# A four-layer kernel on one core: the second expert run and layer 2 put into one instruction stream

## The chip, the cores and the metric

The kernel runs on one core of one Trainium2 chip. The core has five instruction streams: PE (TensorE, matrix products), DVE (VectorE), ACT (ScalarE, functions by table), POOL (GpSimd) and SP (SyncE, which here issues DMAs). Each executes its own instructions in the order in which they were built; semaphores make one wait for another. SBUF is the working memory with 128 partitions. PSUM takes PE's results in eight banks, each holding 128x512 float32 numbers. The metric is the device time of one launch in microseconds; the lower the better.

## What is computed

Eight sequences of 512 tokens with 128 features (`x[0]` to `x[7]`, float32) stay in SBUF and pass through four layers. Each layer has a feed-forward half, an attention or mixing part, and again the feed-forward half. Every part works on a layer-normed copy of `x`, and a feed-forward half adds half of its result. The change touches layer 1's feed-forward (a mixture of experts, which runs twice) and all of layer 2, with the first feed-forward of layer 3. The reference, cut to those:

```python
# layer 1, ffn: 16 experts of width 64, the 4 best of each token
scores = jax.nn.sigmoid(xf @ gate_w.T)
...                     # best 2 of 4 groups, then best 4 experts in them
topk_w = topk_w / (topk_w.sum(-1, keepdims=True) + 1e-20) * SCALE
cw = (jax.nn.one_hot(topk_idx, E) * topk_w[..., None]).sum(1)
hg = jnp.einsum('nh,eih->nei', xf, Wg)
hu = jnp.einsum('nh,eih->nei', xf, Wu)
act = jax.nn.silu(hg) * hu
y = jnp.einsum('nei,ne,ehi->nh', act, cw, Wd)
shared = jax.nn.silu(xf @ Ws_g.T) * (xf @ Ws_u.T) @ Ws_d.T
return x + (y + shared)

# layer 2, ffn: inputs and weights rounded to a 4-bit grid by blocks of 16
h = jax.nn.silu(fp4_linear(x, w_gate)) * fp4_linear(x, w_up)   # width 352
return fp4_linear(h, w_down)

# layer 2, mixing: gates by 16x16 blocks, a product and a sum along the tokens
a = jnp.exp(-8.0 * gate_a * jax.nn.softplus(a_param))
p = jnp.cumprod(a, axis=1)
return p_prefix * jnp.cumsum(x * gate_x * multiplier / p_prefix, axis=1)

# layer 3, ffn: relu(x @ w1 + b1) @ w2 + b2, width 512
```

`cw` is called "shares" here: one number for each token and expert, zero where the expert was not chosen. All 16 experts are computed for all tokens, and the shares select.

## The kernel before

`_run_stages` calls one method after the other: `l0_ffn`, `l0_attn`, `l0_ffn`, `l1_ffn`, `l1_attn`, `l1_ffn`, `layer2`, `l3_attn`, `l3_ffn`. A Tile scheduler turns what they emit into one instruction stream for each engine. The order of emission is the priority, and the scheduler reorders by its own model of when operands are ready. Inside a `with self.in_order(...)` block the named engines keep the order of emission. Each stage opens its own SBUF and PSUM pools and closes them at its end, so a stage's first tiles wait until the stage before has released the space. A tile name with `bufs=n` is a ring of n buffers: the n+1st use waits for the readers of the first.

**The experts.** `routed(b)` prepares sequence b: it norms it (`norm`, lines 322 to 338), transposes it on PE (`transposed`, 421) into `xT`, and `route` computes the scores and the ranks in 26 DVE operations with two POOL operations between them (`ranks`, 947 to 953). Line 1005 ends the shares. Then `routed` splits them into a leading and a trailing part (876, 878), copies both four times side by side on POOL (881), transposes the result on PE (887) and rounds it to fp32r on ACT (891). `experts(b)` does the nine wide products. Eight steps take two experts each, the ninth is the shared one. In each step PE computes `pg` and `pu` (two 128x512 products), ACT takes the silu of `pg` into `act` (913), DVE multiplies by `pu` (914). For each pair of steps PE spreads the shares of four experts over 128 partitions with two small products `pw`, and DVE multiplies `act` by `pw` (922). The product `po` adds up all nine in one bank. At the end the result is copied (929), transposed (932) and added (934, 431). `routed(b + 1)` is emitted between the steps of `experts(b)`.

PSUM holds two banks each of `pg`, `pu` and `pw`, and one each of `po` and `mm`. All products are float32; each 128x512 one is two records of PE in the trace.

Constants that later stages need are prepared between the steps. `attention_constants` runs in the first expert run, `layer2_constants` (with the load of layer 2's weights, their rounding and nine transposes) in the second.

**Layer 2.** `layer2` cuts the three kinds of work into pieces with a slot each: `rounded_ffn` (twice), `recurrence` (two sequences at a time) and `relu_ffn`, layer 3's first feed-forward. A piece's slot is its table entry (`_ROUNDED_FFN`, `_RECURRENCE`, `_RELU_FFN`) plus a start and a step for each sequence (`_STARTS`, `_STEPS`); all pieces are sorted by slot and emitted in that order. Within one rounded ffn, `fp4_in` takes block maxima and scales (1015 to 1027, the last on POOL), `fp4_out` rounds with ACT, two DVE operations and POOL (1040 to 1043), `gated` computes silu and product (1187, 1188), then come transposes (1203) and the down product. A recurrence uses three of ACT's function tables in turn: sigmoid, exp and sqrt. PSUM holds two banks of `mm`, two of `pg`, one of `pu`, one of `po` and two for `big`.

## Time and profile before

| | us |
|---|---|
| device time, median of 3 runs (2458.51 to 5899.11) | 2463.48 |
| the profiled execution | 2460.62 |
| its span, from the first instruction to the last | 2458.9 |
| PE busy in the span, 10967 matmul records | 2156.8 |
| DVE busy, 3830 instructions | 1643.1 |
| ACT busy, 1838 instructions | 1247.7 |
| POOL busy, 923 instructions | 648.8 |
| mean granted PE clock | 0.914 of full |

In the trace the stages lie one after the other: the first expert run from 491 to 750 us, layer 1's attention from 750 to about 1258, the second expert run from there to 1517, layer 2 with layer 3's first ffn from 1517 to 1926, layer 3's attention from there to 2385.

"Busy" is the time in which an engine executes at least one instruction. PE's matrix products are pipelined, so the start-to-start distance of two of them says more than their length: the two records of a 128x512 float32 product last 1.02 us together, and the next product begins 0.86 us after the first at full clock. On DVE, operations that follow each other without a wait overlap by about 0.08 us. The granted clock is either full or half in each interval of the record, and a stage's figure is the mean.

Two instructions that the change concerns show up like this when grouped: the product with `pw` (line 922) 128 times at 682 ns on DVE, and the POOL products of the same shape, 128x512 float32 with both inputs in SBUF, at 1268 to 1329 ns (lines 1285 and 1264).

### The profile page before, as it was taken

The numbers are of one execution on the slowest core, as the hardware profiler recorded it, in microseconds if no ns is written. First come the engines' busy times: TensorE is split into PE (matmuls) and PEld (weight loads), VectorE is DVE, ScalarE is ACT, GpSimd is POOL, SyncE is SP. The second block draws the span as 40 slices with busy tenths as digits, with TensorE's granted clock in tenths as the row PEclk, the third lists the DMA queues.
The fourth block names the chain that finished last, engine by engine and source line by source line (L and its number), as shares of the span: only waits on it lengthen the run. The fifth ranks groups of instructions, "written<-read, shape, count | busy, mean of one in ns | idle before, by whom it ended". The sixth has DMA issues, their size and how long they took to land.

```text
span 2458.9 us, 30169 instructions
## 1 busy us (share of the span) xinstructions
PE 2156.8 (88%) x10967; PEld 1025.0 (42%) x10967; DVE 1643.1 (67%) x3830; ACT 1247.7 (51%) x1838; POOL 648.8 (26%) x923
## 2 busy tenths in 40 slices
PE   7679998889998988899979997877678899999989
PEld 3344444434444333333334443544344444444444
DVE  4566775568777788888538776887675465666611
ACT  3546664323321566777643332566665235555554
POOL 1123442023111011111122112565554013333330
PEclk9779998989997799999979998887899779999999
DMA  3000000000000000000000000000000000000001
GB/s 119 1 1 1 1 1 14 10 0 1 0 0 1 1 1 1 1 1 1 1 7 1 0 1 1 1 1 1 0 1 1 1 1 1 1 1 1 2 1 34
DMA packets 10036, 13.08 MB, mean 5 GB/s; under 512 B 416, under 2 KB 8736, under 8 KB 9760
## 3 DMA queue, kind: packets, MB, share of 16 engines
q1 hardware_dynamic: 7776, 10.11, 1.2%
q8 instruction: 86, 1.41, 0.2%
q10 hardware_dynamic: 2112, 1.05, 0.2%
q14 instruction: 62, 0.51, 0.1%
HBM read 9.06 MB, written 2.10 MB: 5 GB/s over the span
## 4 chain that ended last, share of the span: by engine, by line
PE 60%; DVE 21%; POOL 8%; ACT 7%; issue 4%; DMA 0%; ACTq 0%; DVEq 0%; POOLq 0%; SPq 0%
PE pair L312 11%; PE av L312 8%; PE first L312 7%; PE mm L312 6%; PE po L312 6%; PE pu L312 4%; PE pg L312 4%; DVE max L1595 3%; ACT e L1703 3%; PE ck L312 2%; PE pr L312 2%; PE pw L312 1%; PE ph L312 1%; PE pi L312 1%; PE pf L312 1%
## 5 line engine op out<-in xcount | busy, mean ns | idle before, releaser
L1595 DVE TENSOR_REDUCE max<-first 128x1 f32<-128x512 f32 (+3 forms) x864 | 534.9, 665 | 193.7 <-PE first L312 189.4
L1703 ACT ACTIVATE e<-pair 128x1024 f32<-128x1024 f32 (+3 forms) x512 | 436.4, 864 | 242.3 <-PE pair L312 229.2
L312 PE MATMUL first<-qkT 32*128 32x512 f32 (+3 forms) x1024 | 338.1, 474 | 30.1 <-DVE max L1595 29.4
L312 PE MATMUL pair<-qkT 32*128 32x512 f32 (+3 forms) x1024 | 224.1, 456 | 19.5 <-ACT e L1703 14.4
L312 PE MATMUL av<-e,v 128*32 128x512 f32 (+3 forms) x2048 | 240.1, 538 | 0.1
L913 ACT ACTIVATE act<-pg 128x512 f32<-128x512 f32 x144 | 86.0, 597 | 230.5 <-PE pg L312 179.1
L312 PEld LDWEIGHTS pair<-qkT 32*128 32x128 f32 x1024 | 95.8, 186 | 235.8 <-ACT e L1703 133.5
L312 PE MATMUL pair<-mT,max_rows 32*128 32x512 f32 (+3 forms) x1024 | 192.3, 377 | 1.8 <-DVE mT L1637 1.8
L312 PEld LDWEIGHTS first<-qkT 32*128 32x128 f32 x1024 | 153.1, 198 | 96.0 <-DVE max L1595 87.7
L1705 POOL TENSOR_SCALAR_AFFINE_SELECT e<-e 128x256 f32<-128x256 f32 x256 | 103.4, 407 | 253.3 <-ACT e L1703 253.0
L312 PE MATMUL po<-act,w_moe 128*128 128x512 f32 x288 | 157.1, 632 | 4.4 <-DVE act L922 3.9
L312 PE MATMUL pg<-xT,w_moe 128*128 128x512 f32 x288 | 153.0, 614 | 0.0
L312 PE MATMUL pu<-xT,w_moe 128*128 128x512 f32 x288 | 149.9, 604 | 0.5 <-DVE act L914 0.4
L914 DVE TENSOR_TENSOR act<-act,pu 128x512 f32<-128x512 f32 x144 | 98.3, 683 | 54.5 <-PE pu L312 49.1
L1601 POOL COPY copies<-max 128x128 f32<-128x128 f32 x64 | 22.7, 410 | 343.4 <-DVE max L1595 343.4
L922 DVE TENSOR_TENSOR act<-act,pw 128x512 f32<-128x512 f32 x128 | 87.0, 682 | 17.8 <-PE pw L312 16.2
L312 PEld LDWEIGHTS pair<-mT,max_rows 32*128 32x128 f32 x1024 | 97.3, 189 | 3.6 <-DVE mT L1637 3.3
L951 POOL TENSOR_TENSOR ge<-ge,w_moe 128x64 f32<-128x64 f32 (+1 forms) x32 | 42.7, 1335 | 192.6 <-DVE ge L949 188.7
L1562 ACT CAST qkT<-pair 128x1024 fp32r<-128x1024 f32 x64 | 64.7, 1013 | 41.2 <-PE pair L312 40.6
L312 PEld LDWEIGHTS pu<-xT,w_moe 128*128 128x128 f32 x288 | 53.6, 193 | 65.4 <-issue 58.2
L421 PE MATMUL mm<-w_const,xn 128*128 128x128 f32 x192 | 39.9, 323 | 42.2 <-DVE xn L338 26.4
L312 PEld LDWEIGHTS pg<-xT,w_moe 128*128 128x128 f32 x288 | 52.3, 194 | 54.6 <-issue 54.1
(398 smaller groups left out, 4264.0 us busy)
## 6 DMA issues: line engine op xcount, KB each, us to landing
w_moe<-in_moe SPq DMA_DIRECT2D x1, 2392.0 KB, 14.0
out<-x SPq DMA_DIRECT2D x8, 256.0 KB, 2.3
x<-in_u ACTq DMA_DIRECT2D x4, 256.0 KB, 6.7
x<-in_u SPq DMA_DIRECT2D x4, 256.0 KB, 6.5
w_mixer<-in_l0a SPq DMA_DIRECT2D x1, 960.5 KB, 8.2
w_mixer<-in_l1a SPq DMA_DIRECT2D x1, 769.0 KB, 4.1
w_ffn<-in_l0f SPq DMA_DIRECT2D x1, 578.0 KB, 7.3
w_ffn<-in_l2f SPq DMA_DIRECT2D x1, 560.0 KB, 3.3
```

What stands on the lines that cost most here:

```text
L312: self.nc.tensor.matmul(out, lhsT, rhs, start=start, stop=stop)
L421: self.nc.tensor.transpose(pt[:, c, :], xn[:, c, :], self.ident)
L913: nc.scalar.activation(act, pg, AF.Silu)
L914: nc.vector.tensor_tensor(act, act, pu, ALU.mult)
L922: nc.vector.tensor_tensor(act, act, pw[e % 2], ALU.mult)
L951: nc.gpsimd.tensor_tensor(ge.rearrange(flat), ge.rearrange(flat), self.wide(before, m), ALU.mult)
L1562: self.nc.scalar.copy(t, p)
L1595: nc.vector.tensor_reduce(mx[:, c, j, gs[0] : gs[-1] + 1], sc, AX.X, ALU.max, negate=True)
L1601: nc.gpsimd.tensor_copy(copies[:, :, :, :, g], mx[:, :, :, g].unsqueeze(3).to_broadcast([P, NC, 4, 8]),)
L1703: nc.scalar.activation(e[:, :, :n], sc[:, :, :n], AF.Exp, scale=scale)
L1705: nc.gpsimd.affine_select(e[:, :, :P], e[:, :, :P], pattern=[[0, 2], [1, P]], compare_op=ALU.is_ge, fill=0.0, base=0, channel_multiplier=-1,)
```

## The change

The shares no longer go through PE. `routed` transposes the plain shares to 16x512, copies them to SBUF (`shareT`), writes them by DMA to a 32 KB tile in DRAM, and reads them back by eight DMAs, each of which repeats two rows over 64 partitions. The result is four tiles `share_wide` of 128x2x512 for each sequence, in a ring of four. `experts` multiplies `act` by them: on POOL for the steps 1, 4 and 7, on DVE for the other five. The down product lags two steps behind instead of one, `act` has four buffers instead of three, and `xT` three instead of two. The splitting, the copies, the `pw` products and their weights (1024 columns of the expert pack) are gone. Both expert runs have this.

In the first run the routing is emitted one and a half sequences ahead, and both sets of constants are prepared there, those of layer 2 between the steps of sequences 2 to 6.

The second run and `layer2` become one method, `experts_layer2`, with one list of pieces. The experts take 6.5 slots for each sequence; layer 2's first ffn starts at slot 18. The pieces before slot 7.5 are emitted under `in_order` for POOL and DVE, and the routing of sequences 0 and 1 comes first among them. The recurrence takes one sequence at a time. To fit the eight banks, the experts of this run have one `pu` bank and two `mm`; the down product of the first rounded ffn takes a `mm` bank. Several rings of layer 2 get shorter (`f_xn`, `x_r`, `h` and others from three to two, `hT` from two to one).

```diff
-    p.add("spread", np.tile(np.repeat(np.eye(16, dtype=np.float32), 64, axis=1), (8, 1)))
...
-_STARTS = (0, 7, 32, 40)
-_STEPS = (4, 7, 8, 8)
+_EXPERTS = 6.5
+_IN_ORDER = 7.5
+_STARTS = (18, 27, 46, 64)
+_STEPS = (8, 8, 8, 7)
 _DOWN = [(0, 128), (128, 128), (256, 96)]
 _ROUNDED_FFN = {
     "stats": -10,
-    "apply": -6.5,
-    "x_in": -6,
+    "apply": -7,
+    "x_in": -5,
     "x_out": -4,
     "turned": -1.5,
-    "gated": (0.5, 0.5, 1, 1),
+    "gated": (0, 0, 1, 1),
     "h_in": (0.5, 2),
-    "h_out": (2, 2),
-    "h_turned": (3, 5.5),
-    "down": 6.5,
+    "h_out": (2, 4),
+    "h_turned": (4, 5),
+    "down": 5.5,
 }
...
     def l1_ffn(self):
-        nc, tc = self.nc, self.tc
+        tc = self.tc
         with ExitStack() as s:
-            keep = s.enter_context(tc.tile_pool(name="keep", bufs=1))
-            self.sb = s.enter_context(tc.tile_pool(name="sb", bufs=2))
             self.ps = s.enter_context(tc.tile_pool(name="ps", bufs=2, space=bass.MemoryType.PSUM))
-            self.shares = keep.tile([P, 8, P], F32R, name="shares")
-            nc.vector.tensor_copy(
-                self.shares.rearrange("p e m -> p (e m)"), self.w["moe", "spread"]
-            )
-            self.seqs = [{} for _ in range(NB)]
-            for _ in self.routed(0):
-                pass
+            self.rings = {"mm": 1, "pg": 2, "pu": 2}
+            self.open_experts(s)
+            def all_routed():
+                for b in range(NB):
+                    yield from self.routed(b)
+                    yield
+                    yield
+            ahead = all_routed()
+            for _ in range(15):
+                next(ahead)
             for b in range(NB):
-                ahead = self.routed(b + 1) if b + 1 < NB else iter(())
                 experts = self.experts(b)
                 for step in range(10):
-                    ordered = self.aside_at[0] if b == 1 or (b, step) in self.aside_at[1] else ()
+                    ordered = self.both if (b, step) in self.aside_at else ()
                     with self.in_order(*ordered):
                         next(experts)
                         next(ahead, None)
-                        if (b, step) in self.aside_at[1]:
-                            next(self.aside, None)
-                for _ in ahead:
-                    pass
+                        if (b, step) in self.aside_at:
+                            next(self.aside_at[b, step], None)
+    def open_experts(self, s):
+        tc = self.tc
+        self.sb = s.enter_context(tc.tile_pool(name="sb", bufs=2))
+        self.dram = s.enter_context(
+            tc.tile_pool(name="dram", bufs=2, space=bass.MemoryType.DRAM)
+        )
+        self.seqs = [{} for _ in range(NB)]
     def routed(self, b):
...
         q["xn"] = self.norm(self.x[b], self.ln_pool)
         yield
-        xT = sb.tile([P, L], F32, name="xT")
-        q["xT"] = self.transposed(q["xn"], ps, xT, nc.scalar.copy, bufs=1)
+        xT = sb.tile([P, L], F32, name="xT", bufs=3)
+        q["xT"] = self.transposed(q["xn"], ps, xT, nc.scalar.copy, bufs=self.rings["mm"])
         yield
         out = []
         yield from self.route(xT, sb, ps, out)
         share = out[0]
-        lead = sb.tile([P, NC, 16], F32R, name="share_lead")
-        nc.vector.tensor_copy(lead, share)
-        trail = sb.tile([P, NC, 16], F32, name="share_trail")
-        nc.vector.tensor_tensor(trail, share, lead.bitcast(F32), ALU.subtract)
-        halves = sb.tile([P, NC, 4, 2, 16], F32, name="halves")
-        for k, t in enumerate((lead.bitcast(F32), trail)):
-            nc.gpsimd.tensor_copy(
-                halves[:, :, :, k, :], t.unsqueeze(2).to_broadcast([P, NC, 4, 16])
-            )
+        pt = ps.tile([P, NC, P], F32, name="mm", bufs=self.rings["mm"])
+        for c in range(NC):
+            nc.tensor.transpose(pt[:16, c, :], share[:, c, :], self.ident)
+        shareT = sb.tile([16, L], F32, name="shareT", bufs=1)
+        nc.scalar.copy(shareT, pt[:16].rearrange("p c t -> p (c t)"))
         yield
-        pt = ps.tile([P, NC, P], F32, name="mm", bufs=1)
-        for c in range(NC):
-            nc.tensor.transpose(
-                pt[:, c, :], halves[:, c].rearrange("p r k e -> p (r k e)"), self.ident
-            )
-        q["shareT"] = sb.tile([P, L], F32R, name="shareT")
-        nc.scalar.copy(q["shareT"], pt.rearrange("p c t -> p (c t)"))
+        rows = self.dram.tile([16, L], F32, name="shares")
+        nc.sync.dma_start(out=rows, in_=shareT)
+        pairs = rows.rearrange("(e k) t -> k e t", k=2)
+        for j in range(4):
+            q["share", j] = sb.tile([P, 2, L], F32, name="share_wide", bufs=4)
+            for k in range(2):
+                nc.sync.dma_start(
+                    out=q["share", j][bass.ts(k, 64)],
+                    in_=pairs[k][2 * j : 2 * j + 2].unsqueeze(0).to_broadcast([64, 2, L]),
+                )
         yield
...
-        last = None
+        acts = []
         for e in range(9):
-            pg = ps.tile([P, L], F32, name="pg")
+            pg = ps.tile([P, L], F32, name="pg", bufs=self.rings["pg"])
             self.mm(pg, w("w_g")[:, bass.ts(e, P)] if e < 8 else w("ws_g"), xT)
-            pu = ps.tile([P, L], F32, name="pu")
+            pu = ps.tile([P, L], F32, name="pu", bufs=self.rings["pu"])
             self.mm(pu, w("w_u")[:, bass.ts(e, P)] if e < 8 else w("ws_u"), xT)
-            act = sb.tile([P, L], F32, name="act", bufs=3)
+            act = sb.tile([P, L], F32, name="act", bufs=4)
             nc.scalar.activation(act, pg, AF.Silu)
             nc.vector.tensor_tensor(act, act, pu, ALU.mult)
             if e < 8:
-                if e % 2 == 0:
-                    pw = []
-                    for k in range(e, e + 2):
-                        r = bass.ts(k % 4, 32)
-                        pw.append(ps.tile([P, L], F32, name="pw"))
-                        self.mm(pw[-1], self.shares[r, k, :], q["shareT"][r, :])
-                nc.vector.tensor_tensor(act, act, pw[e % 2], ALU.mult)
-            if last is not None:
-                down(*last)
-            last = (e, act)
+                eng = nc.gpsimd if e in (1, 4, 7) else nc.vector
+                eng.tensor_tensor(act, act, q["share", e // 2][:, e % 2, :], ALU.mult)
+            acts.append((e, act))
+            if len(acts) > 2:
+                down(*acts.pop(0))
             yield
-        down(*last)
-        yT = sb.tile([P, L], F32, name="yT")
+        for last in acts:
+            down(*last)
+        yT = sb.tile([P, L], F32, name="act", bufs=4)
         nc.scalar.copy(yT, po)
-        pt = ps.tile([P, NC, P], F32, name="mm", bufs=1)
+        pt = ps.tile([P, NC, P], F32, name="mm", bufs=self.rings["mm"])
         for c in range(NC):
             nc.tensor.transpose(pt[:, c, :], yT[:, bass.ts(c, P)], self.ident)
-        y = sb.tile([P, NC, D], F32, name="y")
-        nc.vector.tensor_tensor(y, pt, q["xn"], ALU.add)
+        y = q["xn"]
+        nc.vector.tensor_tensor(y, pt, y, ALU.add)
         self.add_half(b, y)
         yield
...
-    def layer2(self):
+    def experts_layer2(self):
         tc = self.tc
         with ExitStack() as s:
-            self.sb = s.enter_context(tc.tile_pool(name="sb", bufs=2))
+            self.fsb = s.enter_context(tc.tile_pool(name="fsb", bufs=2))
             self.ps = s.enter_context(tc.tile_pool(name="ps", bufs=2, space=bass.MemoryType.PSUM))
+            self.rings = {"mm": 2, "pg": 2, "pu": 1}
+            inner = s.enter_context(ExitStack())
+            self.open_experts(inner)
             todo = []
             def put(at, pieces):
                 todo.extend((at + slot, piece) for slot, piece in pieces)
+            def stepped(at, gen, slots):
+                todo.extend((at + slot, partial(next, gen, None)) for slot in slots)
+            def switch():
+                inner.close()
+                self.asb = s.enter_context(tc.tile_pool(name="asb", bufs=2))
             for b in range(NB):
-                put(_STEPS[0] * b, self.rounded_ffn(b))
-                put(_STEPS[2] * b + _STARTS[2], self.rounded_ffn(b))
+                put(_STEPS[0] * b + _STARTS[0], self.rounded_ffn(b, False))
+                put(_STEPS[2] * b + _STARTS[2], self.rounded_ffn(b, True))
                 put(_STEPS[3] * b + _STARTS[3], self.relu_ffn(b))
-                if b % 2:
-                    put(_STEPS[1] * b + _STARTS[1], self.recurrence((b - 1, b)))
-            for _, piece in sorted(todo, key=lambda t: t[0]):
-                piece()
-    def front(self, b, tag, bufs):
-        nc, sb = self.nc, self.sb
+                put(_STEPS[1] * b + _STARTS[1], self.recurrence((b,)))
+            for b in range(NB):
+                stepped(_EXPERTS * b, self.experts(b), [_EXPERTS * k / 10 for k in range(10)])
+                at = _EXPERTS * (b - 1.5) if b > 1 else 100 * b - 1000
+                stepped(at, self.routed(b), [_EXPERTS * k / 10 + .01 for k in range(10)])
+            todo.append((_EXPERTS * NB - .001, switch))
+            todo.sort(key=lambda t: t[0])
+            with self.in_order(*self.both):
+                for at, piece in todo:
+                    if at < _IN_ORDER:
+                        piece()
+            for at, piece in todo:
+                if at >= _IN_ORDER:
+                    piece()
...
-            po = self.ps.tile([P, L], F32, name="po", bufs=1)
+            po = self.ps.tile([P, L], F32, name="po" if second else "mm", bufs=1 if second else 2)
...
-    "l1_ffn",
-    "layer2",
+    "experts_layer2",
...
-    both = mybir.EngineType.Pool, mybir.EngineType.DVE
+    k.both = mybir.EngineType.Pool, mybir.EngineType.DVE
     for at, name in enumerate(_STAGES):
-        if at == 3:
-            k.aside = k.attention_constants(ctx)
-            next(k.aside)
-            k.aside_at = both, [(1, n) for n in range(10)]
-        if at == 5:
-            k.aside = k.layer2_constants(ctx)
-            next(k.aside)
-            k.aside_at = both, [(b, n) for b in range(NB - 1) for n in (3, 8)]
+        if name == "l1_ffn":
+            heads, second = k.attention_constants(ctx), k.layer2_constants(ctx)
+            next(heads), next(second)
+            k.aside_at = {(1, n): heads for n in range(10)}
+            k.aside_at.update({(b, n): second for b in range(2, NB - 1) for n in (2, 5, 8)})
         getattr(k, name)()
     k.store()
```

## What was predicted

> **What bounds the kernel now.** I read the busy time by stage first, then the same by stretches of 25 us, PE's timeline in the expert run, DVE's at that run's start, and the waits of layer 2. By stage (stretch, its length, busy us of PE, weight loads, DVE, ACT, POOL, then granted clock):
>
> ```profile
> 491.00:750.00 259.00, 242.05 (x656) 104.93 (x656) 193.23 (x528) 77.43 (x119) 53.39 (x71) 0.96 0.00 1
> 1256.00:1517.00 261.00, 243.67 (x673) 106.72 (x672) 189.81 (x504) 83.24 (x126) 46.93 (x59) 0.95 0.01 2
> 1517.00:1926.00 409.00, 295.32 (x1186) 178.02 (x1184) 300.17 (x770) 245.21 (x480) 209.65 (x205) 0.86 0.00 1
> ```
>
> Both expert runs are PE's: in the second, 25 us windows between 1330 and 1505 show it busy for 171 of 175 us. Layer 2 belongs to nobody. DVE leads with 73%, and PE, often idle, gets only 0.86 of its clock. So PE time is spare in layer 2 and DVE time in the experts.
>
> A typical stretch of PE in the second run:
>
> ```profile
> 1322.78 1.07 PE L312 MATMUL mm<-w_moe,xT 128*128 128x16 f32 x8
> 1323.78 0.50 PE L312 MATMUL pw<-shareT,shares 32*128 32x512 f32 x2
> 1324.21 1.12 PE L312 MATMUL po<-act,w_moe 128*128 128x512 f32 x2
> 1325.17 1.02 PE L312 MATMUL pg<-xT,w_moe 128*128 128x512 f32 x2
> 1326.03 1.02 PE L312 MATMUL pu<-xT,w_moe 128*128 128x512 f32 x2
> ```
>
> A product's pitch is 0.86 (pg to pu). A pair of `pw` takes 0.43, and the product behind it 0.96, 0.10 more.
>
> The start of that run on DVE, end of the first shares and the first product with them:
>
> ```profile
> 1282.09 0.20 DVE L1005 TENSOR_SCALAR share<-share 128x64 f32<-128x64 f32 x1
> ...
> 1286.04 1.28 DVE L922 TENSOR_TENSOR act<-act,pw 128x512 f32<-128x512 f32 x2 [3.27 <-PE pw L312]
> ```
>
> **pw leaves PE.** 32 pairs in each run at 0.53 make 17 us a run, all on the path in the PE-bound first one. The four share transposes stay (16 rows instead of 128; 0.17 us each now, I take the same). The casts and POOL copies that go lie beside PE.
>
> **The start of the first run.** In the changed program as built, DVE does route(1) up to its two wide comparisons before the first product with shares. In this trace route(0) has its share at 514.33, the first such product is at 518.08. Behind the share I count: transposes and two copies 1.1 + 1.2, a gate product 1.9, sigmoid with its table load 1.5, 16 small DVE operations with one POOL wait 4, two comparisons 2.4, so about 527.5: 9.5 us later, PE mostly idle. The detour by DRAM is not in this trace; by the nearest rows (256 KB land 2.3 us after issue, 560 KB after 3.3) it ends at 514.3 + 1.7 for transposes and copy + 2 x 2.3 = 521, at 2 x 3.3 at 523, and hides behind that. First run: -17 + 9.5 = -7; ends -17 (the delay is made up) and +3 (the pitch of 0.10 stays with other switches). Layer 2's constants come in here, about 15 us of DVE, which has 66 us free, and nine transposes (1.3 us).
>
> **The start of the second run.** Here `in_order` puts the whole of route(0), then all of route(1), ahead of the first product on DVE. How long a routing takes alone the first run shows: from the last statistics (490.44) to the share (514.33) 24 us, less 4 for a cast and three products in between: 20. So the first product comes at 1282.3 + 20 = 1302 instead of 1286. Behind route(1)'s waits on DVE stand the products with `pu`, and for those PE waits with its one `pu` bank. PE then has 22 us of sequence 0 left (25 products at 0.86), and I add 3 for half clock: y(0) at 1327 (now 1313.5). Ends 1320 and 1335.
>
> **Experts with layer 2 beside them.** I counted PE's and DVE's instructions in the built order between one sequence's y and the next. PE at 0.86 for a 512-wide product, 0.59 for a 352-wide (by columns), 0.14 for a transpose, 0.215 for a down product; DVE at this trace's durations less the 0.08 of overlap. The last segment on PE, as an example: 25 expert products and two gates of a recurrence 23, 16 products of `gated` 9.5, 12 down products 2.6, 40 transposes 5.6, together 41. PE: 26, 29, 32, 35, 33, 37, 41 = 233. DVE, where a sequence of experts comes to some 20, a rounded ffn 13, a recurrence 5.5, a relu ffn 2: 28, 28, 30, 36, 35, 35, 36 = 228. The larger of each pair sums to 238. Within them lie about five of 16 rounded ffns and three of eight recurrences. In-order engines that need each other don't reach that. PE in the expert run reaches 0.98, DVE between 1555 and 1830 in layer 2 reaches 0.80; I take 0.88: 270 (243 to 298). y(7) at 1597.
>
> ACT goes from 42 to 60 table loads at 1.28: 23 us more. Its fullest segment is 33 of 41 us, so PE covers them; without cover they cost the 23.
>
> **The rest.** After y(7) by the same count: PE 180 (80 products of `gated` 47, 144 down 31, 74 of 512 columns 63, 276 transposes 39), DVE 184, ACT 170. From 1580 to 1930 DVE is busy for 250 of 350 us, 0.71; with 0.80 at best I take 0.75: 245 (230 to 259; PE's sum at the clock of 0.86 is 209, which at 0.71 gives 294 as the worst). End at 1597 + 245 = 1842 against 1926: -84.
>
> **The products on POOL.** 24 a run, 1.27 to 1.33 each (lines 1285, 1264). On POOL they stand ahead of the rankings' 2.35 us product and layer 2's roundings; each waits for DVE's product with `pu`, and these queue behind. POOL's total in the merged part, 257 + 31 - 7, spreads over 590 us. They save DVE 24 x 0.61, which is in the counts. The other 40 now read both inputs from SBUF instead of one from PSUM, and this row is the same operation, once while POOL's two products ran (until 1621.24) and once after:
>
> ```profile
> 1620.05 1.74 DVE L1288 TENSOR_TENSOR ag<-ag,ig 128x512 f32<-128x512 f32 x1 [3.38 <-POOL ig L1285]
> 1621.82 1.22 DVE L1289 TENSOR_TENSOR_SCAN ig<-ones,ag 128x512 f32<-128x512 f32 x1
> 1622.96 0.67 DVE L1288 TENSOR_TENSOR ag<-ag,ig 128x512 f32<-128x512 f32 x1
> ```
>
> So each of the 40 costs 0 to 0.69 more (mean of line 1288: 1357 ns, free 666). At POOL's share of 281 / 584 = 0.48 I take 0.48 x 0.69 = 0.33: 13 us of DVE in the merged run, which the 0.88 has to hold, and none in the first, where PE leads. The Trainium skill, SBUF — State Buffer, "Who interferes with whom", speaks against this part of the change: a VectorE operation with two SBUF inputs and a GpSimd operation that reads SBUF exclude each other for a whole instruction. The row agrees. If every one of the 40 met a full POOL product of 1.3, that rule would make it 52 us and the forecast some 2410.
>
> **SP.** Nine DMAs a sequence come onto its queue. Ahead of the second run's stands the load of `w_mixer`, which waits for attention's last reader (1267.6), before the first share. `share_wide` for sequence b+1 waits on SP for the products of b; only stores at the end queue behind.
>
> Sum: -7 - 84 = -91. The execution of 2460.6 becomes 2370, the median of 2463.5 becomes **2372**. Ends: 1320 + 243 + 230 = 1793 with -17 gives -150; 1335 + 298 + 259 = 1892 with +3 gives -31.
>
> **Rivals.**
>
> *No room.* Three engines lie within 10% of each other in the rest, and ACT near them late in the experts; the overlap gains little. At layer 2's 0.71: 238 / 0.71 = 335, and PE's 209 at 0.75 = 279, end 1941, +15 - 7 = 2471. For it: DVE's waits in layer 2 are many and short. Against it: the same mix holds 0.80 over 275 us.
>
> *The single pu bank.* Every `pu` of the experts then waits until DVE has read the last. In layer 2, which has one bank, this is the wait (engine and line, waited for, total us, times, longest):
>
> ```profile
> PEld pu L312 <- DVE h L1188: 29.2, 35, 2.0
> ```
>
> Forecast's idle time is 32 us over 63 steps, 0.5 each. If a pair of the routing's wide comparisons (1.23 + 1.22 on DVE) stands before the product in each of the 63, that adds 2.45 x 63 = 154: 2526, slower. It turns slower than before where the added wait passes 91 / 63 = 1.45 each. Against it: the mean here is 0.8, and between two `pu` PE has 1.7 us of `po` and `pg` to do.
>
> *Late shares.* The shares aren't there when needed: one pair of landings, 4.6 us, lost per sequence in both runs, 74 us: 2446. Against it: the loads are issued some 20 us ahead.
>
> *More.* 0.98 and 0.80 hold throughout, and the first run makes up its start: 2313.
>
> **Chances.** Forecast 0.71, more 0.05, no room 0.10, pu bank 0.07, late shares 0.07. What a measurement tells from no change is 2%, 49 us: below 2414. Of the forecast's range some nine tenths lie there: 0.71 x 0.92 + 0.05 = 0.70 faster; slower 0.05 from the bank and 0.03 from no room; the rest 0.22. The range 2318 to 2448 takes in the forecast and late shares, and leaves out the other three but for the lower part of no room, about 0.2.
>
> **What would show it.** No `pw`, a first run of about 250 us. The first product with shares in the second run 20 us after share(0), with PE idle. y to y there 30 to 46 us, PE clock 0.95 or more until y(7). Lines 928 on DVE above 0.68 where POOL is busy. The merged part 585 us long. Wrong: `pu` waiting for line 925 over 1.5 us more each, PE or DVE waiting for `share_wide` in mid-run, a clock below 0.85 in the rest.

## The result, and the profile after

| | before | after |
|---|---|---|
| device time, median | 2461.36 | 2420.95 (2419.63 to 2426.41) |
| ratio, 95% interval | | 0.9844 (0.9821 to 0.9867) |
| the profiled execution | 2460.62 | 2426.41 |
| its span | 2458.9 | 2424.7 |

The kernel became 1.6% faster, 40 us by the medians, where 91 had been forecast: inside the range, but less than half of the gain, and less than the 2% (below 2414) from which the prediction would have called it a difference. One of the four executions before took 5899 us; the ratio leaves it out, which is why 0.9844 stands for 38 us and the medians for 40. The two profiled executions differ by 34 us. Five borders can be found in both traces: DVE's first addition to the scores in either expert run (line 973 of the changed kernel), the last addition `y` of the first run (line 941), and PE's first and last `pair` of the last attention. Lengths in us between them:

| stage | before | after | change | forecast |
|---|---|---|---|---|
| up to the first routing | 499.3 | 498.0 | -1.3 | 0 |
| first expert run | 248.9 | 259.5 | +10.6 | -7 |
| attention of layer 1 | 518.4 | 510.9 | -7.5 | 0 |
| second run, layer 2, layer 3's first ffn | 659.8 | 619.0 | -40.8 | -84 |
| attention of layer 3 | 460.8 | 465.5 | +4.7 | 0 |
| the end | 71.8 | 71.8 | 0 | 0 |

Over the runs of this study the first row lies between 496 and 504 and the fifth between 460 and 466 without any pattern, so the small changes in these two say nothing.

Busy time by stage in the changed kernel (stretch, length, busy us of PE, weight loads, DVE, ACT, POOL, then granted clock):

```profile
491.00:760.00 269.00, 227.34 (x602) 101.94 (x602) 195.80 (x530) 81.75 (x125) 89.88 (x89) 0.91 0.29 64
1260.00:1618.00 358.00, 293.67 (x916) 142.44 (x917) 278.09 (x714) 173.15 (x292) 153.20 (x138) 0.93 0.19 49
1618.00:1887.00 269.00, 212.52 (x862) 129.20 (x861) 188.62 (x488) 174.05 (x328) 130.62 (x127) 0.89 0.00 1
```

The last two stretches are the merged part, 627 us against 670 before. No engine fills it: PE is busy for 81% of it, DVE for 74%. In the first stretch PE has lost its `pw`, and the stretch is longer all the same.

The second run's start, on DVE (start, duration, engine, line; idle time before it in brackets):

```profile
1280.93 0.20 DVE L1012 TENSOR_SCALAR share<-share 128x64 f32<-128x64 f32 x1
...
1296.90 1.22 DVE L959 TENSOR_TENSOR gt<-gt,ge 128x1024 f32<-128x1024 f32 x1 [2.45 <-POOL ge L958]
...
1300.71 0.68 DVE L925 TENSOR_TENSOR act<-act,pu 128x512 f32<-128x512 f32 x1
1301.43 0.69 DVE L928 TENSOR_TENSOR act<-act,share_wide 128x512 f32<-128x512 f32 x1
```

As the prediction had it, all of route(1) stands between the first shares and the first product with them, at 1301.4 (forecast 1302); y(0) follows at 1327.2 (1327). From there y(7) takes 290 us (270), and the rest behind it 270 (245). A typical stretch of PE late among the experts:

```profile
1537.51 1.02 PE L313 MATMUL pu<-xT,w_moe 128*128 128x512 f32 x2
1538.37 1.02 PE L313 MATMUL po<-act,w_moe 128*128 128x512 f32 x2
1540.60 0.86 PE L313 MATMUL pg<-w_gateT,fxT 128*128 128x352 f32 x2 [1.21 <-ACT act L924]
1541.32 1.13 PE L313 MATMUL pu<-xT,w_moe 128*128 128x512 f32 x2
1542.29 1.02 PE L313 MATMUL po<-act,w_moe 128*128 128x512 f32 x2
1544.45 0.86 PE L313 MATMUL pg<-w_gateT,fxT 128*128 128x352 f32 x2 [1.15 <-ACT act L924]
1545.15 1.02 PE L313 MATMUL pg<-xT,w_moe 128*128 128x512 f32 x2
1547.14 0.63 PE L1322 MATMUL mm<-w_const,p 128*128 128x128 f32 x4 [0.97 <-DVE p L1316]
```

Before, these products followed each other at 0.86. Now PE stops after every few of them, here for ACT and for DVE. The five largest of its waits over the merged part from y(0) on (engine and line, waited for, total us, times, longest):

```profile
PE mm L1230 <- POOL h_r L1050: 20.9, 11, 3.5
PE pu L313 <- DVE act L925: 17.6, 13, 4.6
PE pu L313 <- DVE h L1215: 9.4, 14, 1.8
PE mm L1322 <- DVE p L1316: 8.0, 4, 3.3
PE po L313 <- POOL act L928: 5.9, 9, 2.6
```

The largest is POOL's last step of the rounding, and POOL was no term of the forecast's sum.

### The profile page after: what moved, and what is told of

Same layout as the page of the kernel before. It is cut to its first block, busy times and chain, and to the rows that moved or that the text cites. A ratio compares the mean times of both kernels' runs of the same rounds, so it can differ in the third digit from the quotient of the medians.

```text
span 2424.7 us, 29946 instructions
## 1 busy us (share of the span) xinstructions
PE 2098.9 (87%) x10779; PEld 1010.7 (42%) x10839; DVE 1621.2 (67%) x3748; ACT 1271.4 (52%) x1858; POOL 710.3 (29%) x939
## 4 chain that ended last, share of the span: by engine, by line
PE 56%; DVE 23%; POOL 8%; ACT 7%; issue 5%; DMA 0%; ACTq 0%; POOLq 0%; DVEq 0%; SPq 0%
PE pair L313 12%; PE av L313 8%; PE first L313 7%; PE mm L313 7%; PE po L313 5%; DVE max L1621 3%; PE pu L313 3%; ACT e L1729 3%; PE pg L313 3%; PE ck L313 2%; PE pr L313 2%; DVE xn L339 1%; PE ph L313 1%; POOL ge L958 1%; PE pi L313 1%
## 5 line engine op out<-in xcount | busy, mean ns | idle before, releaser
L313 PE MATMUL pu<-xT,w_moe 128*128 128x512 f32 x288 | 155.6, 625 | 15.6 <-DVE act L925 15.5
L928 POOL TENSOR_TENSOR act<-act,share_wide 128x512 f32<-128x512 f32 x48 | 66.3, 1381 | 103.9 <-DVE act L925 96.6
L313 PEld LDWEIGHTS po<-act,w_moe 128*128 128x128 f32 x288 | 53.6, 201 | 98.6 <-issue 31.9
```

Of the source, the lines that this page charges most:

```text
L313: self.nc.tensor.matmul(out, lhsT, rhs, start=start, stop=stop)
L928: eng.tensor_tensor(act, act, q["share", e // 2][:, e % 2, :], ALU.mult)
```

## The experiments

Ratios are to the kernel before, measured beside each run, and have intervals of +-0.001 to +-0.003; 0.001 is 2.5 us. Stages are read from each profiled execution by the borders above: "first run" 259.5 and "merged" 619.0 in the changed kernel, the latter cut at y(7) into 348.5 and 270.5.

### The new shares alone

The kernel before with the changed `routed`, `experts` and `l1_ffn` in both runs; `layer2` and its constants as before.

> The kernel before with the new shares alone (by DRAM, three of eight products on POOL, 15 steps of routing ahead) in both runs; layer 2 and its constants stay where they were. By the prediction's arithmetic (-17 for pw, +9.5 for the start) each run gains 7: 2461 - 14 = 2447, each y(0) to y(7) about 186. By what the trace of the changed kernel shows of its first run (+9, pace 206 from y(0) to y(7)) each run loses 9 instead, and the shares cost 18 in all: 2479. If attention's 7 us gain comes with the first run's new order, 2472.

2455.95, ratio 0.9963. The first run took 243.4: 5.5 less than before, against 7 forecast. From y(0) to y(7) it fell from 202.7 to 189.8, and the start took 7.4 longer. So this term held, and what the changed kernel loses in its first run isn't the shares. Attention gave the gain back: 525.1 instead of 518.4.

### Fewer steps of routing ahead

```diff
-            for _ in range(15):
+            for _ in range(10):
```

> The changed kernel with 10 instead of 15 steps of routing ahead of the first run, so that route(1) starts with the experts of sequence 0. Theory 'route(1) ahead costs the start 9': the first product with shares moves from 527 to about 520, and y(7) of the first run from 757 to about 750, the total to 2414. Rival 'late shares': each sequence's shares are now loaded only as the sequence starts, and 4 to 6 us are lost in each of seven: y(7) later than 770, total 2440 or more.

2433.1, ratio 0.9866, and the first run 270.6. Counted from the first routing its y(0) comes 4 us sooner than in the changed kernel, y(1) 1 later and y(7) 11 later. The steps ahead cost the start 4 and are worth 15 from there on. Neither expectation holds in full. The first product with shares on DVE comes only 0.6 us sooner, because in this trace too the scheduler puts route(1), up to its two wide comparisons, ahead of it; so this run doesn't tell what route(1) costs the start. And the shares do come late with ten steps, here in the first run (waits, as above):

```profile
DVE act L928 <- DMA share_wide<-shares: 19.9, 11, 2.6
POOL act L928 <- DMA share_wide<-shares: 11.9, 8, 2.9
```

The fifteen steps are what keeps the detour by DRAM hidden.

### Layer 2's constants elsewhere, and out of the fixed order

In the first kernel they move to slots 0.5 to 11.7 of the merged part; in the second they stay, and one line changes:

```diff
-            k.aside_at.update({(b, n): second for b in range(2, NB - 1) for n in (2, 5, 8)})
...
+            stepped(0.5, self.second, [0.8 * k for k in range(15)])
```

```diff
-                    ordered = self.both if (b, step) in self.aside_at else ()
+                    ordered = self.both if b == 1 else ()
```

> The changed kernel with layer 2's constants made at the start of the merged part instead of beside the first run. Theory 'the constants, costed at nothing, are what the first run loses' (shares alone, without them, end it at 741.5, the changed kernel at 757.5): y(7) of the first run at about 742, the merged part 5 to 8 longer, total 2411. Rival 'POOL's late products cost the first run, the constants are covered': y(7) stays at 755 or later, total 2421 to 2428.

> The changed kernel with layer 2's constants beside the first run as before, but not held to the order of emission on POOL and DVE. Theory 'their work costs it': the first run stays within 4 of 259.5. Rival 'the order costs it': the first run falls to 245 to 250, total 2408 to 2412.

`consts_merged`: 2415.89, ratio 0.9815; first run 243.4, merged 630.2. The constants cost the first run the 16 us exactly, and 11 where they went. `consts_unordered`: 2408.95, ratio 0.9774 (+-0.003); first run 245.6, merged 617.2. The work is the same, and so are the steps beside which it is emitted: 14 of the 16 us are the price of the order that POOL and DVE are held to. The traces show two ways in which it costs. One is a wait on DVE, in the stretch of these constants, in the changed kernel:

```profile
DVE gt L959 <- POOL ge L958: 9.0, 8, 2.3
DVE xn L339 <- POOL xn_rstd L328: 4.7, 4, 1.5
```

and without the order, where the second of these is below 1 us:

```profile
DVE gt L959 <- POOL ge L958: 3.6, 6, 1.6
```

The other is that the order keeps the constants beside the experts. One of their operations, in the changed kernel and without the order:

```profile
609.43 1.27 DVE L1089 TENSOR_SCALAR limit<-ones,rate_inv 128x512 f32<-128x512 f32 x1
```

```profile
518.60 0.49 DVE L1089 TENSOR_SCALAR limit<-ones,rate_inv 128x512 f32<-128x512 f32 x1
```

Without the order DVE does 9.5 of the constants' 13.7 us before 520, ahead of the first product with shares, where PE is mostly idle, and y(0) comes no later (53.7 us after the first routing in both). With it all of them stand on DVE between 599 and 703. How the 14 us divide between the two isn't shown. The wait alone is no measure: the second run of `shares_only` makes the same constants in the same kind of order, with 8.7 us of the first wait, and takes 195.6 from y(0) to y(7), 6 more than its first run, which makes none of them.

### All products with shares on DVE

```diff
-                eng = nc.gpsimd if e in (1, 4, 7) else nc.vector
+                eng = nc.vector
```

> The changed kernel with all eight products with shares on DVE. Theory 'POOL's products come late': PE's 12 us of waits for them in the first run go, y(0) to y(7) there falls from 206 to about 194; in the merged run DVE gets 24 x 0.68 = 16 us more and y(0) to y(7) grows from 290 by 5 to 12; in all 2415 +- 6. Rival 'DVE bounds both runs, POOL's products earn their 16 us in each': 2440 to 2452, the merged run 16 longer and the first one not shorter.

2407.78, ratio 0.9767: POOL's part in the products, meant to save DVE 24 x 0.61 a run, costs 19 us by the ratios, 13 by the medians and 14 by the two stages. First run 251.0, merged 613.1: shorter in both, though DVE got more work. The rival that DVE bounds both runs is gone. What happens to DVE's operations beside POOL's, in the changed kernel:

```profile
618.63 1.34 DVE L928 TENSOR_TENSOR act<-act,share_wide 128x512 f32<-128x512 f32 x1
...
621.75 2.29 DVE L956 TENSOR_TENSOR ge<-masked 128x1024 f32<-128x1024 f32 x1
...
692.56 1.28 DVE L1011 TENSOR_TENSOR share<-share,total 128x64 f32<-128x64 f32 x1
```

and on POOL at the first two of these places, a step of the constants' rounding and a product with shares:

```profile
618.58 0.84 POOL L1034 TENSOR_TENSOR w_r<-w_ffn,w_inv 128x384 f32<-128x384 f32 x1 [3.36 <-DVE w_inv L1032]
620.77 2.19 POOL L928 TENSOR_TENSOR act<-act,share_wide 128x512 f32<-128x512 f32 x1 [1.36 <-DVE act L925]
```

Undisturbed DVE's three take 0.68, 1.22 and 0.22, and POOL's product 1.27. But the 40 products of DVE in the merged run average 711 ns and those of the first 706, so the term of 0.33 each (13 us) was 0.03 (1 us): they seldom meet POOL. The Trainium skill, SBUF — State Buffer, "Who interferes with whom", has a VectorE operation with two SBUF inputs and a GpSimd operation that reads SBUF exclude each other; these rows agree. The 52 us, for which each of the 40 would have had to meet a full product of POOL, were not there.

Other operations of DVE pay more. Against the median of the same operation in `dve_products`, all of DVE's operations that overlap one of POOL took 19 us longer in the first run of the changed kernel and 10 in that of `dve_products`; in the merged part 40 and 37 (sums over the traces). So POOL's products cost DVE some 9 us in the first run, which got 8.5 shorter without them, and 2 in the merged part, whose 6 us aren't explained by it.

### Two banks for pu

`pu` gets two banks everywhere in the merged part; `big`, the rounding's scratch, goes to SBUF.

```diff
-            self.rings = {"mm": 2, "pg": 2, "pu": 1}
+            self.rings = {"mm": 2, "pg": 2, "pu": 2}
...
-            self.fp4_out(*q["r", half], self.fsb, big=True)
+            self.fp4_out(*q["r", half], self.fsb)
```

> The changed kernel with two banks for pu in the merged part; the two banks come from the rounding's scratch, which moves to SBUF. Theory 'the single bank costs PE what it waits for the product with pu there (17.6 us before y(7), 7 behind it)': y(0) to y(7) of the merged run from 290 to about 272, the rest from 270 to 265, total about 2400. Rival 'the wait is only the place where DVE's lateness shows': within 5 us of 2421, PE waits as long elsewhere.

2418.04, ratio 0.9804 (10 us by the ratios, 3 by the medians); merged 613.5, 5.5 less. PE's waits for line 925 among the experts move from one product to another; two rows of the changed kernel, then of this one:

```profile
PE pu L313 <- DVE act L925: 17.6, 13, 4.6
PE po L313 <- DVE act L925: 1.3, 3, 0.6
```

```profile
PE po L313 <- DVE act L925: 8.1, 3, 3.7
PE pu L313 <- DVE act L925: 6.1, 6, 2.2
```

The bank cost some 5 us, and part of its wait was only the place where DVE's lateness showed.

### What leads the merged part

Three kernels leave work of one engine out of layer 2's rounded ffns, a fourth takes ACT's table changes out of the recurrence (`Exp` and `Sqrt` become `Silu` like the `Sigmoid` shown).

```diff
-                for k, (_, n) in enumerate(_DOWN):
+                for k, (_, n) in enumerate(_DOWN[:1]):
...
-        nc.scalar.activation(big, r, AF.Abs, scale=2.0**22)
-        nc.vector.scalar_tensor_tensor(r, big, 1.5 * 2.0**22, r, ALU.max, ALU.add)
-        nc.vector.scalar_tensor_tensor(r, big, 1.5 * 2.0**22, r, ALU.max, ALU.subtract)
+        nc.scalar.activation(big, r, AF.Abs, scale=1.0 if n != 384 else 2.0**22)
+        if n != 384:
+            nc.vector.scalar_tensor_tensor(r, big, 1.5, r, ALU.max, ALU.subtract)
...
-        nc.gpsimd.tensor_tensor(self.blocks(r), self.blocks(r), self.each(scale), ALU.mult)
+        if r.shape[1] == 384:
+            nc.gpsimd.tensor_tensor(self.blocks(r), self.blocks(r), self.each(scale), ALU.mult)
...
-                    nc.scalar.activation(q[n], pg, AF.Sigmoid, bias=a(n + "_b"))
+                    nc.scalar.activation(q[n], pg, AF.Silu, bias=a(n + "_b"))
```

> The changed kernel with only the first of three terms of each down product in the rounded ffns of layer 2: 128 of 192 products fewer (the output is not the reference's). They take 0.22 each by the forecast's price (28 us) and 0.36 by the changed kernel's trace (46). Theory 'PE leads the merged part: 466 us busy where 413 were counted': 25 to 46 less, total 2375 to 2396. Rival 'order and latency between engines lead': 10 or less, 2411 to 2421.

> The changed kernel with one of the two rounding steps of DVE left out in layer 2 (16 of 0.68 and 32 of 0.88, 39 us; the output is not the reference's). Theory 'PE leads': 5 to 15 less, total 2406 to 2416. Rival 'DVE leads the merged part': 30 to 39 less, 2382 to 2391. If both this and the lighter PE give half of what they remove, the engines take turns and neither leads.

> The changed kernel without the product with the scale on POOL at the end of each rounding in layer 2 (16 of 1.06 and 32 of 1.39, 61 us of POOL, which is busy for less than half the time; the output is not the reference's). Theory 'latency of the rounding: PE's 21 us of waits for this product in the rest': 15 to 25 less, total 2396 to 2406. Rival 'these waits are slack': 5 or less, 2416 to 2421.

> The changed kernel with the recurrence's sigmoids, exponentials and roots replaced by silu, which ACT has loaded already (the output is not the reference's). Some 35 to 45 of the 60 table loads of 1.28 go, 45 to 58 us of ACT. The prediction took ACT's loads as covered: within 5 of 2421. Rival 'they are in the chain like POOL's products': 20 or more less, 2400 or less.

| left out | work, us | merged | change | per us left out | ratio |
|---|---|---|---|---|---|
| PE, 128 down products | 32 | 620.2 | +1.2 | 0 | 0.9859 |
| DVE, 48 rounding steps | 39 | 605.0 | -14.0 | 0.36 | 0.9777 |
| POOL, 48 products with the scale | 61 | 589.4 | -29.6 | 0.49 | 0.9727 |
| ACT, 44 table loads | 56 | 597.0 | -22.0 | 0.39 | 0.9759 |

The 32 of PE are the busy time of the down products, 53.7 us in the changed kernel and 21.7 with the lighter PE; the expectation had put 46. The result is against that expectation, and against the prediction, which left POOL and ACT out of its sum. These pieces of the busiest engine are worth nothing, and those of one that is idle for more than half the time are worth most. Each price is that of the piece and its place: the rounding steps, the products with the scale and the tables stand inside a chain that goes from engine to engine, the down products at the end of one. Other work of PE wasn't left out, so no price of PE as a whole is shown. PE's stretch behind y(7), first with the lighter PE, then in the changed kernel:

```profile
1616.00:1887.00 271.00, 195.63 (x678) 108.02 (x676) 188.38 (x490) 171.32 (x323) 133.97 (x128) 0.87 0.00 1
```

```profile
1617.00:1887.00 270.00, 213.52 (x871) 130.20 (x870) 189.62 (x489) 174.05 (x328) 131.40 (x128) 0.89 0.00 1
```

PE has 193 records less and is busy 18 us less, at a lower clock, in the same 270 us: it was waiting anyway. What it waits for most there (20.9 us, above) is the rounding of `h`, one of which looks like this in the timeline of all engines in the changed kernel:

```profile
1554.32 1.39 POOL L1034 TENSOR_TENSOR h_r<-h,h_inv 128x704 f32<-128x704 f32 x1 [2.25 <-DVE h_inv L1032]
...
1555.74 0.76 ACT L1047 ACTIVATE big<-h_r 128x704 f32<-128x704 f32 x1 [1.10 <-POOL h_r L1034]
1556.53 0.89 DVE L1048 SCALAR_TENSOR_TENSOR h_r<-big,h_r 128x704 f32<-128x704 f32 x1 [0.19 <-ACT big L1047]
...
1557.77 0.88 DVE L1049 SCALAR_TENSOR_TENSOR h_r<-big,h_r 128x704 f32<-128x704 f32 x1
1558.79 1.39 POOL L1050 TENSOR_TENSOR h_r<-h_r,h_scale 128x704 f32<-128x704 f32 x1 [3.09 <-DVE h_r L1049]
```

Each step starts as the one before ends, or behind one other operation on its engine: 5.9 us from POOL by ACT and DVE back to POOL, with DVE ahead of it and PE's transposes behind. POOL itself stood idle for 3.09 us before the last step. A sequence has six such roundings, and a recurrence that goes back and forth in the same way.

ACT's loads in the merged part of the changed kernel by line (count, busy, mean ns), for the recurrence's lines:

```profile
L1286 ACT ACT_TABLE_LOAD x8 | 10.3, 1283 | 0.1
L1292 ACT ACT_TABLE_LOAD x8 | 10.3, 1283 | 0.1
L1307 ACT ACT_TABLE_LOAD x8 | 10.3, 1283 | 0.1
```

The Trainium skill, ScalarE: Activation LUTs, "What ACT_TABLE_LOAD costs", adds about 1.38 us of drain to each load's 1.28. This trace shows the 1.28, and no such drain: of the 59 loads between 1268 and 1887, 57 begin within 0.02 us of the end of the operation before, and 44 are followed within 0.02 us by the next operation (the other 15 of these wait for PE or POOL). Here the measurement decides. In the stage's time a load was worth 0.5 us (22 us for 44), less than its own length.

### The prices put to the test

```diff
-        nc.gpsimd.tensor_tensor(self.blocks(r), self.blocks(r), self.each(scale), ALU.mult)
+        eng = nc.gpsimd if n == 384 else nc.vector
+        eng.tensor_tensor(self.blocks(r), self.blocks(r), self.each(scale), ALU.mult)
```

> The changed kernel with the product with the scale that ends each rounding of layer 2 on DVE instead of POOL. The lighter runs gave prices for the merged part: 30 us for 61 of POOL (0.49 each), 14 for 39 of DVE (0.37 each), 0 for 46 of PE. Theory 'the part is led by hops between in-order queues, and these are the prices': -61 x 0.49 + 39 x 0.37 = -15, total 2405. Rival 'DVE leads once it gets more': +20 to +39, 2440 to 2460. Rival 'only that the work is gone made the runs lighter, not the hop': 2421 +- 4.

Merged 604.9: -14.1, for the -15 that the prices gave. The total moved less, 2417.47, ratio 0.9821 (+-0.003); the profiled execution shows 7 us more in the stages ahead of the merged part, of which the edit touches only one rounding of constants (128x352). So the prices hold for pieces of the chain in which they were found, and the total doesn't tell this edit from no change.

### Overlap, or layer 2's new form?

`_STARTS = (64, 73, 92, 110)` puts all of layer 2's pieces behind the experts. `shallow` cuts the rings in the old `layer2`, on top of the kernel with the new shares alone; `deep_hTr` sets `hT` to 2 and `h_r` to 3 buffers in the changed kernel.

> The changed kernel with layer 2's start put behind the experts, so that its new form runs alone. From y(7) to the last attention the old form takes 409 to 412. Theory 'the new form is slower by itself (shallower rings, recurrences one at a time)': 425 to 440 there, the merged part 619 + 55 to 70, total 2475 to 2490. Rival 'the form is as good, the overlap costs': 405 to 412, total 2455 to 2465.

> The kernel before with the new shares (the run shares_only: 2456, layer 2 there 411.5) with layer 2's rings cut as in the change: f_xn, x, fxT, h, h_r from 3 to 2, hT from 2 to 1. Theory 'the rings cost': layer 2 takes 420 to 435, total 2465 to 2480. Rival 'they are slack': 409 to 414, total 2456.

> The changed kernel with hT's ring back at 2 and h_r's at 3. Theory 'the rings cost': the rest behind y(7) 8 to 20 shorter than 270, total 2400 to 2412. Rival 'slack': 267 to 271, total 2421.

`no_overlap`: 2459.55, ratio 0.9994 (+-0.001). Its experts, then its layer 2:

```profile
1319.00:1508.00 189.00, 177.73 (x481) 77.66 (x482) 138.24 (x354) 67.74 (x113) 56.42 (x51) 0.99 0.30 71
1508.00:1910.00 402.00, 294.83 (x1183) 178.75 (x1181) 288.33 (x720) 247.70 (x471) 205.95 (x194) 0.87 0.00 1
```

The new form alone is as good as the old one (402.7 behind y(7); 411.5 with the new shares, 409.1 before). Put side by side the two take 655.2; overlapped, 619.0. The overlap is worth 36 us, where the forecast needed some 80, and that is the whole shortfall of the merged part.

`shallow`: 2466.56, ratio 1.0020 (+-0.001); layer 2 took 416.9 instead of 411.5, while the total is 11 above that of the new shares alone. `deep_hTr`: 2422.85, ratio 0.9851, merged 614.2. Both stages show 5 us of the rings, less than expected; the totals disagree with each other, so their price is not settled beyond that it is small.

### Versions that beat both

`combo1` joins `dve_products`, `pu2` and `consts_merged`; `combo2` joins `dve_products`, `pu2` and `round_out_dve`; `combo3` all four; `combo12` is `combo2` with `consts_unordered`.

> The changed kernel with all products with shares on DVE, two banks for pu in the merged part, and layer 2's constants there. Singly they gave 19, 10 and 7 by their ratios. If each takes away another wait they add up: 2385. If two of them meet in the same wait (DVE's late product with pu), some half: 2400.

> The changed kernel with all products with shares on DVE, two banks for pu, and the roundings' last product on DVE too. POOL then has some 100 us in the merged part and DVE 480 of 560. By the prices: 2421 - 19 - 10 - 15 = 2377. Rival 'DVE leads now': 2400 or more, DVE busy for over 90% of the stretch from y(0) to y(7).

> The changed kernel with all four: products with shares on DVE, two banks for pu, the roundings' last product on DVE, layer 2's constants in the merged part. By the stages of the single runs: first run 233 to 235 (combo1), merged part 598 (combo2) + 4 for the constants (combo1's 611 against some 607), together 2396 - 18 + 4 = 2382. Rival 'the constants meet a DVE that is now full': merged 612 or more, total 2390 or more.

> The changed kernel with products with shares on DVE, two banks for pu, the roundings' last product on DVE, and layer 2's constants left beside the first run but not held to the order of emission. If the costs are independent: first run 259.5 - 14 - 8 to 10 = 236 to 238, merged part 598, together 2396 - 14 = 2382. Rival 'DVE is full in the first run too once it has all the products and the constants': first run 245 or more, total 2390 or more.

| | us | ratio, interval | first run | merged |
|---|---|---|---|---|
| combo1 | 2394.87 | 0.9731 (0.9710 to 0.9752) | 233.4 | 611.3 |
| combo2 | 2395.86 | 0.9735 (0.9710 to 0.9761) | 251.5 | 598.1 |
| combo3 | 2389.09 | 0.9695 (0.9665 to 0.9724) | 233.4 | 601.9 |
| combo12 | 2382.30 | 0.9665 (0.9652 to 0.9678) | 236.1 | 596.2 |

`combo12` is 3.35% faster than the kernel before, at the 2382 expected, and its stages are the 236 to 238 and 598 expected. `combo1` and `combo2` missed 2385 and 2377, which were sums of the single ratios (and, in `combo2`, of a price), each with an interval of some 5 us. By the stages little is lost: the first run and the merged part of `combo1` are together 34 us shorter than in the changed kernel, where the single runs sum to 25, and those of `combo2` 29, where they sum to 32. `combo3` has the stages expected of it, and a median 7 us above its 2382. The busy times of `combo12` by stage:

```profile
494.00:740.00 246.00, 219.29 (x601) 99.12 (x601) 202.39 (x560) 81.54 (x126) 53.06 (x63) 0.93 0.32 72
1250.00:1580.00 330.00, 281.37 (x932) 142.11 (x931) 295.28 (x732) 171.16 (x292) 94.67 (x87) 0.95 0.21 52
1580.00:1849.00 269.00, 205.88 (x846) 129.06 (x845) 211.18 (x530) 173.37 (x330) 103.65 (x101) 0.90 0.00 1
```

DVE is busy for 0.89 of the middle stretch (0.78 in the changed kernel). There it comes near to being full; in the last stretch still nobody is, and its length is that of the changed kernel.

## Why the prediction was right and wrong, step by step

**pw leaves PE (-17), start of the first run (+9.5), together -7.** Right: DVE's first product with shares came at 527.1 (527.5), behind the work that was named, and with the shares alone the first run is 5.5 shorter. Two details are off. The terms listed for the start add up to 526.4, and the second comparison took 2.29 instead of 1.22, beside a product of POOL. And the parts missed in opposite directions: the start cost 7.4 by y(0), and from y(0) to y(7) the run gained 12.9, where 17 were counted for the whole of it.

**Layer 2's constants beside the first run, at nothing.** Wrong, and the first of the two mis-sized terms: +16 (shown by `consts_merged`), of which 14 are the fixed order on POOL and DVE (`consts_unordered`). The prediction counted 15 us of work against 66 free us. The steps are emitted under `in_order`, as the diff shows, and the prediction costed the order only at the second run's start.

**The second run's start.** Right to a microsecond, 1301.4 and 1327.2. Of the other signs that were named, PE's clock from y(0) to y(7) was 0.97, as forecast; y to y took 31 to 50 us, not 30 to 46, and the merged part 619 by its borders, not 585.

**Experts with layer 2 (270) and the rest (245).** Wrong by 20 and 25, the second term: the larger of PE's and DVE's sums, divided by 0.88 and 0.75. The factors stood for "engines that need each other", but the sum took its size from the engines' loads. With the prediction's own sums they came out as 0.82 and 0.68. Of what was left out, PE's down products weigh 0, DVE's rounding steps 0.36, ACT's table loads 0.39, POOL's products with the scale 0.49: what costs time is work in chains from engine to engine and in queues behind it, which the sum didn't have. PE's sums were also too low (413 counted, 466 busy); `pe_light` speaks against that as the cause. The rival "no room" came nearest to this step (several engines, not one, and a gain of overlap that is small); its own number, 2471, overshot, because its 0.71 on 238 made 335 of what took 290.

**Table loads, 18 more, covered by PE's longer segments.** Wrong: 44 loads fewer gave 22 us, so by that price 18 loads cost some 9 (an estimate; no run had the recurrences in pairs beside the experts).

**The products on POOL.** The price of shared reading on DVE's 40 products was 1 us for 13, as above; what it cost DVE's other operations, some 9 us in the first run, had no term. What POOL's products were to save was counted as saved, and is not: taking them away gains 13 to 19.

**SP and the shares by DRAM, hidden.** Right. The one wait for `share_wide` in the trace is 2.4 us, on POOL, once; the rival of late shares is out for this kernel, and real with ten steps ahead (`ahead10`).

**The single pu bank.** The rival's price was 2.45 a step; PE waits for line 925 there 17.6 us over 63 steps, 0.3 each, and a second bank gives 5.5 in all.

**Not foreseen: attention, -7.5.** See the last section; it makes the miss smaller, by luck.

Of the 91 us, 34 came in the profiled execution. Of the 57 that are missing, 18 are the first run's (16 of them the constants), 43 the merged part's, 3 stages that the change doesn't touch, and 7 came back in attention. What stays open is how the merged part's loss divides between length of the chains and queueing behind other work on POOL, DVE and ACT: the runs that took work out shorten both.

## What to carry to other kernels

When two stages that leave each engine some room are merged, don't divide the largest load by a factor: take a little work out of each engine in turn and see what the time does, since a piece of the busiest engine can be worth nothing and one of an engine at 47% the most. Choose pieces inside the chains as well as at their ends. An order that is forced on an engine has a price wherever an instruction in it waits for another engine, and wherever it keeps work out of a stretch that is idle, not only at the place for which it was made. An engine that is free is no place for a step in the middle of a chain if its operation takes twice as long there and others queue behind.

## What the runs showed of the hardware beyond that

A DVE operation of 128x64 elements, 0.22 us, took 0.84 to 1.29 in four of 16 cases, three beside a product with shares on POOL and one beside a step of the rounding there (line 1011 above); with no product with shares on POOL all 16 took 0.20 to 0.23. Here short operations lost more to POOL than the long ones that were feared for.

Attention of layer 1 took 518.4, 510.9 and 525.1 us in the kernel before, the changed one and the one with the shares alone, though its own work is the same. It is DVE that it waits for most, and the scheduler moves statistics of the second expert run into it: of two, one and seven sequences. DVE's groups in that stretch, in this order of the kernels (count, busy, mean | idle before):

```profile
L322 DVE BATCH_NORM_STATS2 xn_st<-x 128x6 f32<-128x128 f32 x8 | 2.0, 273 | 4.6 <-POOL x L1776 4.6
```

```profile
L323 DVE BATCH_NORM_STATS2 xn_st<-x 128x6 f32<-128x128 f32 x4 | 1.1, 268 | 2.3 <-POOL x L1802 2.3
```

```profile
L321 DVE BATCH_NORM_STATS2 xn_st<-x 128x6 f32<-128x128 f32 x28 | 6.9, 274 | 18.0 <-POOL x L1781 18.0
```

The statistics themselves are short, but each sequence's wait of 2.3 to 2.6 us for POOL's last addition stops DVE in the middle of attention. For the slowest of the three this fits: PE's waits for DVE's row maxima are 25.7, 25.1 and 38.6 us. Between the first two they differ by 0.6 only, and another thing does too: the granted clock, 0.912 before and 0.922 in the changed kernel. Among runs with the same one sequence of statistics in this stage it took 507.3 us at a clock of 0.930 (`combo12`) and 512.9 at 0.917 (`deep_hTr`); by that slope, an estimate, the clock makes some 4 of the 7.5 us. None of this was tried by itself.
